# Four selective-scan layers on one core: x_dbl on both halves of the partitions, dt's projection of two blocks as one pair of matmuls, delta's second half by a transfer

## The chip, the cores and the metric

The kernel runs on one core of a Trainium2 chip. The metric is the device time of one launch in microseconds (us), which processes a batch of eight images. All data are float32.

## The reference

The reference takes x of shape 8 x 64 x 64 x 96 through four residual layers, `x = x + layer(groupnorm(x))`. Each layer is a Mamba block with 192 inner channels and 16 states: an input projection into xpart and z, a depthwise convolution (3x3 in layers 0 to 2, three causal taps in layer 3), SiLU, a selective scan over the 4096 pixels, a gate by silu(z) and an output projection. Layers 0 to 2 scan in four directions (rows and columns, each forwards and backwards; layer 1 in serpentine order) and have a layer norm ahead of the gate; layer 3 scans once. For one direction, cut to what matters:

```python
x_dbl = einsum('bdl,cd->bcl', xs, x_proj_w)          # rank + 16 + 16 rows
dts, B, C = split(x_dbl)
delta = softplus(einsum('brl,dr->bdl', dts, dt_proj_w) + dt_proj_b)
h = exp(delta_t * A) * h + (delta_t * u_t) * B_t     # per channel and state, step by step
y_t = sum over states of h * C_t;  y = y + D * u
```

The rank is 16 in layer 0 and 6 in the others.

## The kernel before, in words

A loop over the eight images holds the four layers, written out (`layer`, L165). A layer has a part ahead of the scans (normalisation, projection, convolution), the scans (`scans`, L600), and a part after them (norm, gate, output projection). The scans are most of the time.

**Chunks and steps.** A direction's 4096 positions are 8 chunks of 512 (CH). `walk` lists the pairs of direction and chunk in order: directions 0, 2, 1, 3 in layers 0 to 2 (32 chunks a layer), one direction in layer 3 (8 chunks). The 192 channels are three tiles t of 64. A tile of h has 64 channels times 2 states on its 128 partitions, so 16 states are 8 rows of scans, in two groups g of 4 (NH). One chunk is one step of 24 slots (SL), one scan each.

**One slot** (loop at L1019, m counts the slots): `scan` (L861) is DVE's recurrence over 512 positions, h = d_a * h + dbu. `decay` (L850), on ACT, computes d_a = exp(delta * A) four slots ahead. `enter` (L828), on PE, in every second slot, multiplies du by the diagonals of B, 16 matmuls on 64x64 tiles, for two scans. In every fourth slot `keep` (L881), on ACT, copies the last column of four scans as the next chunk's state, and `read_out` (L888), on POOL, then multiplies the four scans' h by C in place. `add_up` (L892), on PE, in the odd slots, sums h * C over the states. So six read-outs a step; the third belongs to g = 0, t = 2, the last to g = 1, t = 2.

**Preparation of the next chunk** is spread over the slots of a step by the dictionary `plan` (L935): slot -> functions, with how many chunks ahead they work. `project` (L659) makes x_dbl on PE (rows 0 to 15 C, 16 to 31 B, then a row for the bias and the rank's rows; in layers 0 to 2 the backward direction's rows too, on partitions from 64), for directions 0 and 1. `keep_x_dbl` (L670) copies it out of PSUM on ACT and issues transfers of it to memory: cm (C, which is read back with copies) and xm (all rows of the backward direction). For directions 2 and 3 `load_x_dbl` (L684) reads xm back. `turn_v` (L707) is dt's projection: for each of four blocks of 128 positions (every fourth one, `block`, L703) a matmul of x_dbl's block, as the stationary operand on 39 or 49 rows, with dt's weights gives v (positions on partitions, 192 + 16 columns); e counts pairs of blocks, each with a PSUM bank of its own, b the block in the pair. `turn_u` (L724) transposes u. `softplus` (L733), `keep_b` (L744) and `diagonals` (L780) are ACT's, `delta_of` (L750) and `du_of` (L761) DVE's, `diagonal` (L767) POOL's. `turn_back` (L805) turns delta_t back to channels on partitions, on PE: rows 0 to 127 (o = 0), and rows 128 to 191 (o = 1) twice, for both halves of the partitions. `keep_delta` (L817) copies the three tiles of delta out of PSUM on ACT: each of 64 rows, on both halves of the partitions. `spread_c` (L694) reads C of one group of states from memory with 64 copies of each row, two transfers of 512 KB. `load_u` (L649) reads u, 256 and 128 KB. `close_sums` (L913), on DVE, adds the chunk's sums to y.

**What sets the order.** The order of PE, DVE, ACT and POOL is the program's (`manual_schedule`, L218). SP issues all transfers, and its order is the tile framework's planner's, which goes by the time at which, by its reckoning, a transfer's inputs and buffer are ready, with the program's order as the priority. Buffers (L127 on): c 3, u 4, x_dbl 2, d_a 6, delta 6, and in PSUM 2 for dbu and 2 (`mm`) shared by x_dbl, v, u_t and delta_ps in turn. With three c buffers the second group's c of the next chunk takes the buffer that the third read-out of the present chunk has just read. The fourth u buffer comes free with close_sums of slot 14.

Of the kernel before, what the change touches and what calls it, by code (L numbers as in the profile page):

```python
# [22 lines left out]
F32 = mybir.dt.float32  # L23
# [7 lines left out]
DI = 192  # L31
NS = 16
# [3 lines left out]
CH = 512  # L36
# [128 lines left out]
def layer(tc, env, x, x_of, x_to, n, ly):  # L165
# [191 lines left out]
    def make_ys():  # L357
        return [big.tile([128, L], F32, tag=f"big{o}", name=f"y{o}") for o in range(2)]

    work = scans(  # L360
        tc, env, n, ly, w, u_mem, lambda half: u_chunk(half, 0), d, neg_a, make_ys, mm, wide
    )
# [237 lines left out]
def scans(tc, env, n, ly, w, u_mem, u_first, d, neg_a, make_ys, mm, wide):  # L600
# [7 lines left out]
    nc = tc.nc  # L608
    const, small = env.const, env.small
# [2 lines left out]
    R, K = ly.rank, ly.dirs  # L612
    XP = 33 + R
    RS, SL = 6, 24

    def mem(tag, k, rows):
        return env.dram.tile([rows, L], F32, tag=tag, name=f"{tag}{k}_{n}", bufs=2)
# [3 lines left out]
    x_mem = {k: mem("xm", k, XP) for k in range(2, K)}  # L621
# [5 lines left out]
    us, dbls, cs, diags, turned, rests, deltas = {}, {}, {}, {}, {}, {}, {}  # L627
# [10 lines left out]
    def bank(i, name, part=0):  # L638

        if i > 0:  # L640
            return mm(name)
        if part == 0:
            banks[name] = wide(name)
        return banks[name][:, part * CH : part * CH + CH]
# [25 lines left out]
    def keep_x_dbl(i):  # L670


        k, c = walk[i]
        if k >= 2:
            return
        s = slice(c * CH, (c + 1) * CH)
        x_dbl = small.tile([128, CH], F32, tag="x_dbl", name="x_dbl")[0 : ly.x_rows]
        nc.scalar.activation(x_dbl, dbls[i], AF.Identity, bias=const[0 : ly.x_rows, ONE : ONE + 1])
        nc.sync.dma_start(c_mem[k][:, s], x_dbl[0:NS])
        if K > 1:  # L680
            nc.sync.dma_start(x_mem[k + 2][:, s], x_dbl[64 : 64 + XP])
        dbls[i] = x_dbl[0:XP]

    def load_x_dbl(i):  # L684
        if i >= len(walk):
            return
        k, c = walk[i]
        if k < 2:
            return
        x_dbl = small.tile([128, CH], F32, tag="x_dbl", name="x_dbl")[0:XP]  # L690
        nc.sync.dma_start(x_dbl, x_mem[k][:, c * CH : (c + 1) * CH])
        dbls[i] = x_dbl

    def spread_c(i, g):  # L694
        k, c = walk[i]
# [7 lines left out]
    def block(b, ap):  # L703

        return ap[:, b::NB4]

    def turn_v(i, e, b):  # L707

        if e == 0 and b == 0:
            for name in ("delta_t", "du_t"):  # L710
                turned[i, name] = env.turned.tile([128, NB4, DI], F32, tag=name, name=name)
        if b == 0:
            v = bank(i, "v", e)[:, 0 : 2 * (DI + NS)]
            turned[i, e, "v"] = v.rearrange("p (b d) -> p b d", b=2)
        at = ly.dt_w + walk[i][0] * (DI + NS)
        nc.tensor.matmul(  # L716
            turned[i, e, "v"][:, b],
            block(2 * e + b, dbls[i]),
            w[0:XP, at : at + DI + NS],
            start=True,  # L720
            stop=True,
        )

    def turn_u(i, e, b):  # L724

# [78 lines left out]

    def turn_back(i, o, part):  # L805


        if part == 0:
            deltas[i, "ps", o] = bank(i, "delta_ps", o)
        for b in (2 * part, 2 * part + 1):  # L810
            of = turned[i, "delta_t"][:, b]
            for half in range(o + 1):
                to = deltas[i, "ps", o][64 * half : 64 * half + 128 // (o + 1)]
                of_ = of[:, 0:128] if o == 0 else of[:, 128:DI]
                nc.tensor.matmul(block(b, to), of_, ident, start=True, stop=True)  # L815

    def keep_delta(i, t):  # L817
        delta = env.deltas.tile([128, CH], F32, tag="delta", name="delta")
        if t == 2:
            nc.scalar.copy(delta, deltas[i, "ps", 1])  # L820
        else:
            for half in range(2):
                of = deltas[i, "ps", 0][64 * t : 64 * t + 64]
                nc.scalar.copy(delta[64 * half : 64 * half + 64], of)  # L824
        deltas[i, t] = delta
# [87 lines left out]
    def close_sums(i, o):  # L913
# [21 lines left out]
    plan = {  # L935
        0: [(load_u, 2)],
        1: [(keep_x_dbl, 1)],
        2: [(turn_v, 1, 0, 0)],
        3: [(turn_v, 1, 0, 1)],
        4: [(keep_b, 1, 0), (softplus, 1, 0, 0)],  # L940
        5: [(softplus, 1, 0, 1)],
        6: [(softplus, 1, 0, 2), (diagonal, 1, 0), (turn_u, 1, 0, 0), (spread_c, 1, 0)],
        7: [(turn_u, 1, 0, 1)],
        8: [(delta_of, 1, 0)],
        9: [(turn_v, 1, 1, 0)],
        10: [(diagonal, 1, 1), (turn_v, 1, 1, 1), (close_sums, -1, 0)],
        11: [(keep_b, 1, 1), (softplus, 1, 1, 0)],
        12: [(softplus, 1, 1, 1), (du_of, 1, 0)],
        13: [(softplus, 1, 1, 2), (turn_u, 1, 1, 0), (diagonal, 1, 2)],
        14: [(turn_u, 1, 1, 1), (close_sums, -1, 1)],  # L950
        16: [(delta_of, 1, 1), (spread_c, 1, 1)],
        17: [(turn_back, 1, 0, 0), (diagonal, 1, 3)],
        18: [(turn_back, 1, 0, 1), (du_of, 1, 1)],
        19: [(keep_delta, 1, 0), (load_x_dbl, 2)],
        20: [(turn_back, 1, 1, 0), (keep_delta, 1, 1)],
        21: [(turn_back, 1, 1, 1)],
        22: [(project, 2, 0)],
        23: [(project, 2, 1), (keep_delta, 1, 2)],
    }

    done = 0
    for slot, n_ in (
        *((10, 2), (14, 2), (15, 3), (16, 2), (17, 3), (18, 2), (21, 2), (22, 2)),
        *((24, 2), (25, 1), (26, 2), (27, 2), (28, 1), (29, 1), (30, 1), (31, 2), (32, 2)),
    ):
        plan.setdefault(slot % SL, []).append((diagonals, 1 - slot // SL, done, n_))
        done += n_


    def first_project():  # L970
        project(0, 0)
        project(0, 1)
        keep_x_dbl(0)
        for g in range(2):
            spread_c(0, g)

    def first_turn():
        for do in (turn_v, turn_u):
            for e in range(2):
                for b in range(2):  # L980
                    do(0, e, b)

    def first_softplus(between=lambda: None):
        for e in range(2):
# [21 lines left out]
    def first_load():  # L1006
# [3 lines left out]
    yield SimpleNamespace(  # L1010
        project=first_project,
        turn=first_turn,
        softplus=first_softplus,
        turn_back=first_back,
        keep_delta=first_delta,
# [3 lines left out]
    for m in range(-4, (len(walk) + 1) * SL):  # L1019
        i, slot = divmod(m, SL)  # L1020
# [9 lines left out]
        if slot % 2:  # L1030
            of, e = divmod(m - 13, SL)
# [26 lines left out]
def pack(ly, conv_w, win, conv_b, x_proj, dt_w, dt_b, a_log, d, w_out, gamma=None, beta=None):  # L1058
    K, R = ly.dirs, ly.rank
    XP = 33 + R  # L1060
    a = np.zeros((128, ly.width), np.float32)
    a[0:C, ly.win_x : ly.win_x + DI] = win[:DI].T
    a[0:C, ly.win_z : ly.win_z + DI] = win[DI:].T
    x_proj = x_proj.reshape(K, R + 2 * NS, DI)
    for k in range(K):

        w = x_proj[k].T
        at = ly.x_proj + k % 2 * 2 * ly.x_rows + k // 2 * 64
        for half, rows in enumerate((slice(0, 128), slice(128, DI))):
            to = a[0 : len(w[rows]), at + half * ly.x_rows : at + half * ly.x_rows + XP]  # L1070
            to[:, 0:NS] = w[rows, R + NS :]
            to[:, NS : 2 * NS] = w[rows, R : R + NS]
            to[:, 33:] = w[rows, :R]

        at = ly.dt_w + k * (DI + NS)
        a[32, at : at + DI] = dt_b.reshape(K, DI)[k]
        a[33:XP, at : at + DI] = dt_w.reshape(K, DI, R)[k].T
        for half in range(2):
            for j in range(NJ):
                a[NS + half * NJ + j, at + DI + j // NH * NJ + half * NH + j % NH] = 1  # L1080
    a_log = a_log.reshape(K * NT, 64, 2, NJ).transpose(2, 1, 0, 3).reshape(128, -1)
    a[:, ly.a_log : ly.a_log + K * NT * NJ] = a_log
    d = d.reshape(K, DI)
    a[:, ly.d : ly.d + K] = d[:, :128].T
    a[0:64, ly.d + K : ly.d + 2 * K] = d[:, 128:].T
    conv_w = conv_w.reshape(DI, ly.taps)
    a[:, ly.conv_w : ly.conv_w + ly.taps] = conv_w[:128]
    for p in (0, 64):
        a[p : p + 64, ly.conv_w + ly.taps : ly.conv_w + 2 * ly.taps] = conv_w[128:]
    for v, at in ((conv_b, ly.conv_b), (gamma, ly.gamma), (beta, ly.beta)):  # L1090
        if v is not None:
            a[:, at] = v[:128]
            a[0:64, at + 1] = a[64:128, at + 1] = v[128:]
    a[:, ly.w_out : ly.w_out + C] = w_out[:, :128].T
    for p in (0, 64):
        a[p : p + 64, ly.w_out + C : ly.w_out + 2 * C] = w_out[:, 128:].T
    return a
# [39 lines left out]
```

## Time and profile before

| what | value |
|---|---|
| median of 3 runs | 31,737.26 us (31,715.66 to 31,752.72) |
| the profiled execution's own time | 31,703.4 us |
| its span, first to last instruction | 31,698.6 us |
| PE busy | 30,814.0 us (97%) |
| DVE busy | 28,392.2 us (90%) |
| POOL busy | 27,178.5 us (86%) |
| ACT busy | 26,085.1 us (82%) |
| 16 DMA engines, share of their time | 33.3% in SP's queue |
| read_out, POOL, L890 | 4,992 x 4.557 us |
| scan, DVE, L872 | 19,968 x 1.20 to 1.26 us |
| decay, ACT, L858 | 19,968 x 0.716 us |
| turn_v, PE, L716 | 6,656 records, 8 a step |
| keep_delta, ACT, L824 and L820 | 3,328 x 0.580 us and 832 x 0.586 us |

A matmul of float32 leaves two records, each with a record of its weight load (PEld). Records of matmuls on different tiles of the array overlap, so what a matmul costs is read from start to next start. The clock granted to PE is 0.98 of full speed over the span. In a timeline, columns are start, duration, engine, line, operation, names, and in brackets the engine's idle time ahead of it and what ended it.

### The profile page before, as it was taken

What the parts mean: (1) busy time and instruction counts of PE and PEld (TensorE: products, weight loads), DVE (VectorE), ACT (ScalarE), POOL (GpSimd) and SP (SyncE); (2) the same over time, 40 slices, a digit from 0 to 9 for tenths busy, and PEclk for the clock granted to TensorE, in tenths of its full rate; (3) what the DMA queues carried; (4) which work ended last, traced back from release to release, by engine and by line L of the source; (5) the groups of instructions that cost most, each with busy time, mean ns of one, the idle gap of its engine ahead of it and who ended that gap; (6) DMA issues with size and microseconds to landing.
All of it is one profiled execution on the core that took longest, in us unless ns stands there. A gap on an engine that the chain in (4) does not pass through costs nothing. (4 is left out here: it accounts for less than half of the span.)

```text
span 31698.6 us, 951914 instructions
## 1 busy us (share of the span) xinstructions
PE 30814.0 (97%) x402320; PEld 16776.3 (53%) x402320; DVE 28392.2 (90%) x29432; ACT 26085.1 (82%) x65064; POOL 27178.5 (86%) x9436
## 2 busy tenths in 40 slices
PE   9999999999999999999999999999999999999999
PEld 5555555555555545555455554555555555555555
DVE  9899898998989989899898998989989899898998
ACT  8788788887888878888788887878878888788887
POOL 8898788987889879898798987989878898788987
PEclk9999999999999999999999999999999999999999
DMA  3333233333333333333333333333323333333332
GB/s 90 78 76 85 72 90 79 75 86 73 89 80 74 87 72 88 80 74 87 73 88 80 74 87 74 87 79 74 87 72 89 80 74 86 72 90 79 75 86 72
DMA packets 1262156, 2544.89 MB, mean 80 GB/s; under 512 B 108560, under 2 KB 129296, under 8 KB 1234832
## 3 DMA queue, kind: packets, MB, share of 16 engines
q1 hardware_dynamic: 1257872, 2483.64, 33.3%
q8 instruction: 3192, 52.30, 0.7%
q14 instruction: 1092, 8.95, 0.1%
HBM read 2208.74 MB, written 274.46 MB: 78 GB/s over the span
## 5 line engine op out<-in xcount | busy, mean ns | idle before, releaser
L890 POOL TENSOR_TENSOR h<-h,c 128x2048 f32<-128x2048 f32 x4992 | 22723.0, 4557 | 1867.5 <-ACT state L886 625.9
L872 DVE TENSOR_TENSOR_SCAN h<-d_a,state,dbu 128x512 f32<-128x512 f32 x17472 | 21076.5, 1261 | 1130.2 <-PE dbu L841 687.9
L858 ACT ACTIVATE d_a<-delta,neg_a 128x512 f32<-128x512 f32 x19968 | 14166.5, 716 | 122.1 <-DVE h L872 101.3
L841 PE MATMUL dbu<-diag,du_t 64*64 64x128 f32 x319488 | 11142.2, 277 | 296.4 <-DVE h L872 224.7
L841 PEld LDWEIGHTS dbu<-diag,du_t 64*64 64x64 f32 x319488 | 8712.0, 133 | 5111.5 <-issue 4681.5
L904 PE MATMUL y_ps<-h,const 128*64 128x512 f32 x39936 | 10827.0, 617 | 119.1 <-POOL h L890 110.5
L786 ACT ACTIVATE diag<-const,bt 128x64 f32<-128x64 f32 x25600 | 7550.4, 344 | 14.0 <-PE dbu L841 7.8
L773 POOL TENSOR_TENSOR diag<-const,bt 128x512 f32<-128x512 f32 x3328 | 3475.2, 1045 | 335.0 <-ACT bt L747 246.3
L872 DVE TENSOR_TENSOR_SCAN h<-d_a,dbu 128x512 f32<-128x512 f32 x2496 | 2881.8, 1203 | 498.6 <-ACT d_a L858 216.2
L904 PEld LDWEIGHTS y_ps<-h,const 128*64 128x64 f32 x39936 | 2065.6, 135 | 1899.4 <-issue 1498.5
L716 PE MATMUL v<-w,x_dbl 39*128 39x208 f32 (+1 forms) x6656 | 2618.4, 477 | 8.3 <-DVE delta_t L752 7.3
L716 PEld LDWEIGHTS v<-w,x_dbl 39*128 39x128 f32 (+1 forms) x6656 | 1787.2, 317 | 1568.3 <-issue 883.1
L824 ACT COPY delta<-delta_ps 64x512 f32<-64x512 f32 x3328 | 1930.9, 580 | 566.7 <-PE delta_ps L815 519.6
L815 PEld LDWEIGHTS delta_ps<-const,delta_t 128*64 128x64 f32 (+1 forms) x19968 | 1637.0, 154 | 1415.7 <-issue 949.7
L815 PE MATMUL delta_ps<-const,delta_t 128*64 128x128 f32 (+1 forms) x19968 | 2223.8, 286 | 11.6 <-issue 11.6
L747 ACT COPY bt<-v 128x32 f32<-128x32 f32 x1664 | 300.8, 183 | 1848.7 <-PE v L716 1846.5
L730 PEld LDWEIGHTS u_t<-const,u 128*128 128x128 f32 x3328 | 650.1, 195 | 1583.2 <-issue 887.2
L886 ACT COPY state<-h 128x4 f32<-128x4 f32 x4992 | 972.4, 195 | 568.0 <-DVE h L872 527.9
L454 POOL TENSOR_TENSOR acc<-acc,more 128x512 f32<-128x512 f32 x576 | 756.7, 1317 | 699.6 <-ACT more L453 356.1
L730 PE MATMUL u_t<-const,u 128*128 128x128 f32 x3328 | 1292.2, 388 | 0.0
L320 PE MATMUL conv<-xn,taps 96*128 96x512 f32 (+1 forms) x2496 | 1160.0, 658 | 22.1 <-DVE taps L203 22.1
L731 PE MATMUL u_t<-const,u 64*128 64x64 f32 x3328 | 1098.8, 330 | 0.0
(99 smaller groups left out, 16194.5 us busy)
## 6 DMA issues: line engine op xcount, KB each, us to landing
c<-cm SPq DMA_DIRECT2D x1792, 512.0 KB
c<-xm SPq DMA_DIRECT2D x1536, 512.0 KB
u<-u SPq DMA_DIRECT2D x1088, 256.0 KB
u<-u SPq DMA_DIRECT2D x1088, 128.0 KB
u<-u SPq DMA_DIRECT2D x48, 1024.0 KB
x_mem<-x SPq DMA_DIRECT2D x48, 768.0 KB
x<-x_mem SPq DMA_DIRECT2D x48, 768.0 KB
x<-in_x_dram SPq DMA_DIRECT2D x32, 768.0 KB
```

What stands on the lines that cost most here:

```text
L320: nc.tensor.matmul(part, taps[:, t, d0 : d0 + nd], rhs, start=t == 0, stop=t == ly.taps - 1)
L716: nc.tensor.matmul(turned[i, e, "v"][:, b], block(2 * e + b, dbls[i]), w[0:XP, at : at + DI + NS], start=True, stop=True,)
L730: nc.tensor.transpose(to[:, b, 0:128], block(b_, u_of(i, 0)), ident)
L773: nc.gpsimd.tensor_tensor(diags[i, 0][:, b], sel.unsqueeze(1).unsqueeze(3).to_broadcast([128, NH, 64, 2]), of.unsqueeze(2).to_broadcast([1 ...
L786: nc.scalar.activation(diags[i, 1][:, b, q // 2, :, q % 2], sel, AF.Copy, scale=turned[i, b // 2, "b"][:, b % 2, NJ + q : NJ + q + 1],)
L815: nc.tensor.matmul(block(b, to), of_, ident, start=True, stop=True)
L824: nc.scalar.copy(delta[64 * half : 64 * half + 64], of)
L841: nc.tensor.matmul(to[64 * half : 64 * half + 64, e, b], du[rows, b, 64 * t : 64 * t + 64], diag[rows, b, 2 * half + pair], start=True, st ...
L858: nc.scalar.activation(d_a, deltas[i, t], AF.Exp, scale=neg_a[:, at : at + 1])
L872: nc.vector.tensor_tensor_scan(hs[s][:, m4, flow], decays.pop(m)[:, flow], p[:, flow], 0.0 if first else states[i // NCH][:, j : j + 1], A ...
L890: nc.gpsimd.tensor_tensor(hs[s], hs[s], cs[i, g], ALU.mult)
L904: nc.tensor.matmul(sums[i][o][64 * half : 64 * half + 64], sel, hs[of][:, state, :], start=g == 0 and e in (0, 4), stop=g == 1 and e in (3 ...
```

## The change

x_dbl is kept on two places: on partitions 0 on, and on partitions 64 on. For directions 0 and 1 of a chunk after the first, a transfer makes the second place (x_hi, one buffer); for directions 2 and 3 a second load from xm does. `turn_v` then issues, for one b, the matmuls of both e, one on the rows from 0, one on those from 64, where dt's weights stand a second time. `turn_back` of rows 128 to 191 fills one half of the partitions. `keep_delta` copies each tile of 64 rows to one half only and issues a transfer of that half to the other. The plan deals the preparation anew. The first chunk of a layer has no second place and keeps the old way for delta.

```diff
@@ keep_x_dbl
         nc.scalar.activation(x_dbl, dbls[i], AF.Identity, bias=const[0 : ly.x_rows, ONE : ONE + 1])
+        dbls[i] = [x_dbl[0:XP], x_dbl[0:XP]]
+        if i > 0:
+            there = small.tile([128, CH], F32, tag="x_hi", name="x_hi", bufs=1)[64 : 64 + XP]
+            nc.sync.dma_start(there, x_dbl[0:XP])
+            dbls[i][1] = there
         nc.sync.dma_start(c_mem[k][:, s], x_dbl[0:NS])
         if K > 1:
             nc.sync.dma_start(x_mem[k + 2][:, s], x_dbl[64 : 64 + XP])
-        dbls[i] = x_dbl[0:XP]
@@ load_x_dbl
-        x_dbl = small.tile([128, CH], F32, tag="x_dbl", name="x_dbl")[0:XP]
-        nc.sync.dma_start(x_dbl, x_mem[k][:, c * CH : (c + 1) * CH])
-        dbls[i] = x_dbl
+        x_dbl = small.tile([128, CH], F32, tag="x_dbl", name="x_dbl")
+        dbls[i] = [x_dbl[o : o + XP] for o in (0, 64)]
+        for to in dbls[i]:
+            nc.sync.dma_start(to, x_mem[k][:, c * CH : (c + 1) * CH])
@@ turn_v, now turn_v(i, b)
-        nc.tensor.matmul(
-            turned[i, e, "v"][:, b],
-            block(2 * e + b, dbls[i]),
-            w[0:XP, at : at + DI + NS],
-            start=True,
-            stop=True,
-        )
+        for e, of in enumerate(dbls[i]):
+            o = 64 if i > 0 and e else 0
+            nc.tensor.matmul(
+                turned[i, e, "v"][:, b],
+                block(2 * e + b, of),
+                w[o : o + XP, at : at + DI + NS],
+                start=True,
+                stop=True,
+            )
@@ turn_back
-            for half in range(o + 1):
+            for half in range(o + 1 if i == 0 else 1):
@@ keep_delta
         delta = env.deltas.tile([128, CH], F32, tag="delta", name="delta")
-        if t == 2:
+        if i > 0:
+            here = halves[t % 2]
+            nc.scalar.copy(delta[here], deltas[i, "ps", t // 2][here])
+            nc.sync.dma_start(delta[halves[1 - t % 2]], delta[here])
+        elif t == 2:
             nc.scalar.copy(delta, deltas[i, "ps", 1])
@@ plan
         1: [(keep_x_dbl, 1)],
-        2: [(turn_v, 1, 0, 0)],
-        3: [(turn_v, 1, 0, 1)],
-        4: [(keep_b, 1, 0), (softplus, 1, 0, 0)],
-        5: [(softplus, 1, 0, 1)],
-        6: [(softplus, 1, 0, 2), (diagonal, 1, 0), (turn_u, 1, 0, 0), (spread_c, 1, 0)],
-        7: [(turn_u, 1, 0, 1)],
-        8: [(delta_of, 1, 0)],
-        9: [(turn_v, 1, 1, 0)],
-        10: [(diagonal, 1, 1), (turn_v, 1, 1, 1), (close_sums, -1, 0)],
-        11: [(keep_b, 1, 1), (softplus, 1, 1, 0)],
-        12: [(softplus, 1, 1, 1), (du_of, 1, 0)],
-        13: [(softplus, 1, 1, 2), (turn_u, 1, 1, 0), (diagonal, 1, 2)],
+        3: [(turn_v, 1, 0)],
+        4: [(turn_v, 1, 1)],
+        5: [(keep_b, 1, 0), (softplus, 1, 0, 0), (spread_c, 1, 0)],
+        6: [(softplus, 1, 0, 1), (softplus, 1, 0, 2), (diagonal, 1, 0)],
+        7: [(keep_b, 1, 1), (softplus, 1, 1, 0)],
+        8: [(delta_of, 1, 0), (softplus, 1, 1, 1)],
+        9: [(turn_u, 1, 0, 0), (softplus, 1, 1, 2)],
+        10: [(turn_u, 1, 0, 1), (diagonal, 1, 1), (close_sums, -1, 0)],
+        11: [(delta_of, 1, 1)],
+        12: [(du_of, 1, 0)],
+        13: [(turn_u, 1, 1, 0), (diagonal, 1, 2)],
         14: [(turn_u, 1, 1, 1), (close_sums, -1, 1)],
-        16: [(delta_of, 1, 1), (spread_c, 1, 1)],
-        17: [(turn_back, 1, 0, 0), (diagonal, 1, 3)],
-        18: [(turn_back, 1, 0, 1), (du_of, 1, 1)],
-        19: [(keep_delta, 1, 0), (load_x_dbl, 2)],
-        20: [(turn_back, 1, 1, 0), (keep_delta, 1, 1)],
-        21: [(turn_back, 1, 1, 1)],
+        15: [(turn_back, 1, 0, 0)],
+        16: [(turn_back, 1, 0, 1), (du_of, 1, 1), (spread_c, 1, 1)],
+        17: [(keep_delta, 1, 0), (diagonal, 1, 3)],
+        18: [(keep_delta, 1, 1)],
+        19: [(turn_back, 1, 1, 0), (load_x_dbl, 2)],
+        20: [(turn_back, 1, 1, 1)],
+        21: [(keep_delta, 1, 2)],
         22: [(project, 2, 0)],
-        23: [(project, 2, 1), (keep_delta, 1, 2)],
+        23: [(project, 2, 1)],
@@ slots and numbers of ACT's 32 diagonals (slots from 24 on are those of the chunk's own step)
-        *((10, 2), (14, 2), (15, 3), (16, 2), (17, 3), (18, 2), (21, 2), (22, 2)),
-        *((24, 2), (25, 1), (26, 2), (27, 2), (28, 1), (29, 1), (30, 1), (31, 2), (32, 2)),
+        *((10, 2), (11, 3), (12, 2), (13, 3), (14, 2), (15, 2), (16, 2), (19, 2), (20, 1), (22, 2)),
+        *((23, 2), (24, 1), (26, 2), (27, 2), (28, 2), (31, 1), (32, 1)),
@@ pack
+        a[64 : 64 + XP, at : at + DI + NS] = a[0:XP, at : at + DI + NS]
```

More of the change, by code (lines that the diff above doesn't have):

```diff
@@ L614, in scans @@
     RS, SL = 6, 24
+    halves = [slice(0, 64), slice(64, 128)]
     def mem(tag, k, rows):
@@ L705, in block, with turn_v @@
         return ap[:, b::NB4]
-    def turn_v(i, e, b):
-        if e == 0 and b == 0:
+    def turn_v(i, b):
+        if b == 0:
             for name in ("delta_t", "du_t"):
                 turned[i, name] = env.turned.tile([128, NB4, DI], F32, tag=name, name=name)
-        if b == 0:
-            v = bank(i, "v", e)[:, 0 : 2 * (DI + NS)]
-            turned[i, e, "v"] = v.rearrange("p (b d) -> p b d", b=2)
+            for e in range(2):
+                v = bank(i, "v", e)[:, 0 : 2 * (DI + NS)]
+                turned[i, e, "v"] = v.rearrange("p (b d) -> p b d", b=2)
         at = ly.dt_w + walk[i][0] * (DI + NS)
-        nc.tensor.matmul(
-            turned[i, e, "v"][:, b],
-            block(2 * e + b, dbls[i]),
-            w[0:XP, at : at + DI + NS],
-            start=True,
-            stop=True,
-        )
+        for e, of in enumerate(dbls[i]):
[7 more added lines that the diff above has]
+            )
     def turn_u(i, e, b):
@@ L977, in first_turn @@
     def first_turn():
[L978 to L981, printed above, removed]
+        for b in range(2):
+            turn_v(0, b)
+        for e in range(2):
+            for b in range(2):
+                turn_u(0, e, b)
     def first_softplus(between=lambda: None):
```

## The prediction

> **What bounds the kernel now.** First I read the busy shares of the page (PE 97%, DVE 90%, POOL 86%, ACT 82%): too close together to name one bound. So I timed the steps, by the start of every 24th scan on DVE. They are regular: 33.96 us where the chunk being prepared has x_dbl projected (directions 0 and 1), 33.53 in layer 3, 31.89 where x_dbl is loaded (directions 2 and 3). The 100 steps of an image that are followed by another (31 in each of three layers, 7 in the last) are 800 in the run and take 26,516.7 us, 33.15 on average, of 31,698.6. The change acts there. The engines' busy times over one step of each kind:
> ```profile
> 4670.64:4704.60 33.96, 33.96 (x477) 18.94 (x477) 31.51 (x30) 29.65 (x77) 31.28 (x11) 1.00 0.30 79
> 4934.92:4966.80 31.88, 31.88 (x474) 18.41 (x472) 31.40 (x31) 28.86 (x76) 31.15 (x11) 1.00 0.33 73
> ```
> Columns: stretch, its length, then PE, PEld, DVE, ACT, POOL, clock, DMA share, GB/s. PE is never idle and is the bound, but DVE and POOL stand within 0.5 to 0.8 us of it in the second kind. The timeline of PE around dt's projection:
> ```profile
> 4675.54 1.10 PE L841 MATMUL dbu<-diag,du_t 64*64 64x128 f32 x32
> 4676.57 0.79 PE L716 MATMUL v<-w,x_dbl 49*128 49x208 f32 x2
> 4677.30 1.08 PE L904 MATMUL y_ps<-h,const 128*64 128x512 f32 x4
> 4678.31 0.80 PE L716 MATMUL v<-w,x_dbl 49*128 49x208 f32 x2
> 4679.03 1.10 PE L841 MATMUL dbu<-diag,du_t 64*64 64x128 f32 x32
> ```
> From start to next start a v matmul costs 0.73 us, four a step. The second thing to see is the transfer queue. SP issues, in one step:
> ```profile
> 4694.30 1.23 SPq L700 DMA_DIRECT2D c<-cm  x2
> 4695.63 0.55 SPq L655 DMA_DIRECT2D u<-u  x1
> 4696.22 1.54 SPq L656 DMA_DIRECT2D u<-u  x1
> ```
> POOL tells why c goes out just then, and ACT what POOL waits for:
> ```profile
> 4689.70 4.57 POOL L890 TENSOR_TENSOR h<-h,c 128x2048 f32<-128x2048 f32 x1 [0.35 <-POOL diag L773]
> ...
> 4701.04 4.55 POOL L890 TENSOR_TENSOR h<-h,c 128x2048 f32<-128x2048 f32 x1 [0.26 <-ACT state L886]
> 4706.50 4.55 POOL L890 TENSOR_TENSOR h<-h,c 128x2048 f32<-128x2048 f32 x1 [0.92 <-PE y_ps L904]
> ```
> ```profile
> 4700.81 0.72 ACT L858 ACTIVATE d_a<-delta,neg_a 128x512 f32<-128x512 f32 x1
> 4701.55 1.18 ACT L824 COPY delta<-delta_ps 64x512 f32<-64x512 f32 x2
> ...
> 4706.17 0.20 ACT L886 COPY state<-h 128x4 f32<-128x4 f32 x1
> ```
> The third read-out of a step ends at 4694.27; call that moment t. It frees the c buffer, and c's second half for the next chunk is issued at t + 0.03. The first decay of the next chunk (4700.81) is six us later, and the state copy of 4706.17 must precede the last read-out (4706.50), which overwrites h. The table of waits has both dependencies in total:
> ```profile
> SPq L700 <- POOL h L890: 13914.7, 1475, 17.0
> POOL h L890 <- ACT state L886: 625.9, 1106, 5.2
> ```
> How long the queue is then full is in the DMA column:
> ```profile
> 4702.00:4704.00 2.00, 2.00 (x38) 1.26 (x38) 2.00 (x3) 1.96 (x6) 2.00 (x1) 1.00 0.72 221
> 4704.00:4706.00 2.00, 2.00 (x22) 0.66 (x14) 1.94 (x3) 1.98 (x5) 1.59 (x1) 1.00 0.00 0
> ```
> c and u are moved from 4696 to 4704. By the trace's completion records, over 656 steps: the second c transfer is complete 9.40 us after t, u's first 10.06, u's second (128 KB) 10.70 (9.74 to 11.93 in nine of ten).
>
> **What the Trainium skill says.** "DMA: Bandwidth & Descriptors", section "Queues, rings and completion order": SP owns one ring on each of the DMA engines, and an engine consumes its ring's descriptors in order. The trace agrees: u, issued 1.3 us after c, completes 0.66 us after it and not earlier. "TensorE: Matmul & The Clock Gate", Part 3 ("Packing small matmuls"): matmuls on different row groups run concurrently. Here the 32 records of a dbu group, 0.27 us each, fill 1.03 us on four 64x64 tiles. The same page, Part 1, "Architectural detail": ACT's queue is a strict FIFO; in the timelines here its instructions follow one another in the program's order.
>
> **The change, part by part.**
> - v for two blocks side by side: four matmuls of 0.73 become two pairs. If a pair takes as long as one, -1.45 us of PE a step; if it runs in sequence, 0. I take -1.45, on dbu's evidence.
> - turn_back of rows 128 to 191 to one half: 8 matmuls become 4. The 8 went as column pairs, so little is saved: 0.5 us a part now, 0.64 for the unpaired 128-row parts; between 0 and -0.5 a step, I take -0.05.
> - keep_delta: 4 copies of 580 ns and one of 586 become 3 of 580: -1.17 us of ACT a step. Added: three transfers of 128 KB on SP's queue (about 0.55 us of issue each, SP is free for most of a step) and, for every decay, a wait on their landing.
> - x_dbl's second copy, directions 0 and 1: one transfer ahead of cm and xm, which move back by one issue (0.3 us; c's first half, which needs cm, waits longer for POOL). A write of xm, the same rows, completes 1.93 us after issue (median; 3.13 at nine in ten). In the step shown SP issues cm at 4674.71, as soon as ACT ends x_dbl. Without a v in slot 2, slot 3's y_ps starts at 4676.57 and takes 1.01, so the pair is due at 4677.6. So 2.9 us stand against 1.9 to 3.2: cost 0, bounded by 0.3 us on such steps. What hides it is PE's work of slots 1 to 3; an ACT that comes late takes that away, and then dbu and y_ps queue behind the pair on PE, and DVE waits for dbu. x_hi has one buffer, free since the pairs of the step before have read it. Not less than 0: nothing waited for in slot 2 now goes away on the path. Directions 2 and 3: a second load next to the first, early in the step, 0.
> - The rest of the plan (u's transposes, softplus, diagonals: 32 on ACT as before, POOL's in the same slots): same work in other slots, 0 while PE, DVE and ACT have it in hand a slot before its reader. c's first half is asked for in slot 5 instead of 6, but waits for POOL's last read-out as before. The larger weights' rows: same transfer, 0.
> - **Delta by transfer, in the queue.** keep_delta(t=0) moves from slot 19 to 17, its reader, the first decay of the next chunk, stays in slot 20. SP's order is the planner's. It already puts the u load (slot 0 of the next step, buffer free at slot 14's close_sums) behind c (slot 16), so the planner holds c ready by slot 14; delta, ready at slot 17 at the earliest, then goes behind c, and likely behind u. It lands at t + 10.70 + 0.64 (another 128 KB, u1 to u2) = t + 11.34, with 0.1 for the signal D = t + 11.4. The other two transfers land behind, and are needed four and eight decays later: no wait. The first decay stands at t + 6.5 now. So ACT waits about 5 us, and behind it in ACT's order are, up to the state copy: four decays at 0.62 from start to start, five diagonals at 0.235, one delta copy at 0.55 = 4.2 us. State copy to read-out start is 0.33. So the last read-out starts at t + 15.95, and POOL, which is free at t + 11, idles. From there POOL's own chain runs to the next t: four read-outs at 4.51 and two diagonals at 1.0 = 20.1. **The loop closes at 36.05 us**, for both kinds of step, whatever PE saves: PE (32.5 or 30.4), DVE (31.4) and POOL (31.2) all fit within.
>
> Sum: 800 x 36.05 = 28,840 against 26,516.7: +2,323 us. On the profiled execution's 31,703.4 us that is 34,027; the median of the runs lies 34 us above that execution, so **34,060 us**. Last steps of a layer and all before the scans stay as they are.
>
> **The rivals.**
> 1. The loop, but delta ahead of u in SP's order: D = t + 9.40 + 0.64 + 0.1 = t + 10.15, period 34.8, 800 x 34.8 = 27,840, time 33,060. For it: program order. Against: the planner's readiness (it already lets the x_dbl load of slot 19 go ahead of c of slot 16).
> 2. **Faster:** delta gets ahead of c in SP's queue, or lands early for another reason, and the loop stays open. Then PE's saving counts: steps with projection 33.96 - 1.5 = 32.5, the others fall to DVE's 31.4 with some 0.2 for friction, 31.6. 52 of the former at -1.4 and 48 of the latter at -0.3 (now 31.89) make -88 us an image, -704 in all: 31,030. It decides at D: the period is D - t + 24.65, equal to the present mean of 33.15 at D = t + 8.5. Against it: c alone takes 9.40.
> 3. The pairs do not run side by side: alone, no gain and no loss (31,700); with the loop nothing is changed, since PE has 2 us to spare.
> 4. ACT's lateness reaches x_dbl, and PE waits for its second copy in slot 3: in the loop, keep_x_dbl ends 2.2 us after the state copy's start (a state copy, two decays, a diagonal and itself), at D + 6.4, and the copy lands at D + 8.4; scans then end about 1.7 us ahead of POOL's need. It adds up to 0.3 us to some steps, within the range.
>
> **How the numbers follow.** Loop with u ahead of delta (34,060): 0.60. Loop without (33,060): 0.15. A shorter loop, slower yet than now (31,800 to 32,700): 0.05. Open loop, faster: 0.18. Within 0.2%, about what a measurement of this kernel can tell from no change, and rival 3 with an open loop: 0.02; rival 4 lies within the loop's cases. The first case's own spread is the landing's, -0.4 to +0.7 us a step, 33,750 to 34,600. A range of 32,500 to 34,700 holds the first two and most of the third, 0.79.
>
> **What would show it.** Right: steps of one length, near 36, in both kinds; ACT's decay waiting for the delta transfer some 5 us a step; POOL's last read-out waiting for ACT's state copy; PE with 3 to 5 us idle in a step; v pairs at about 0.75 us. Wrong: SP's order with delta ahead of c; steps of 32.5 and 31.6; no ACT wait on the transfer.

## The result, and the profile after

The changed kernel takes 35,533.39 us (median of 4 runs, 35,515.51 to 35,554.03) against 31,740.61 us of the kernel before in the same session (4 runs): ratio 1.1196, 95% interval 1.1179 to 1.1212. It is slower, as forecast, but by 3,793 us and not by 2,323: the time lies 833 us above the top of the range.

| us | before | after |
| --- | --- | --- |
| span of the profiled execution | 31,698.6 | 35,535.1 |
| the 800 steps of the prediction | 26,516.7 (33.15 each) | 30,293.7 (37.87 each) |
| all the rest | 5,181.9 | 5,241.4 |
| clock granted to TensorE, of full speed | 0.980 | 0.932 |

So 3,777 of the 3,837 us more are in the steps. On the page of the changed kernel, the busy times of the engines are close to what they were, but their shares are not, and two groups have long waits ahead of them (after the bar: busy time, mean, then the idle time and what ended it):
```profile
PE 31916.4 (90%) x395920; PEld 16858.1 (47%) x395920; DVE 28475.2 (80%) x29432; ACT 25186.5 (71%) x63464; POOL 27089.7 (76%) x9436
...
L871 ACT ACTIVATE d_a<-delta,neg_a 128x512 f32<-128x512 f32 x19968 | 14186.6, 715 | 4909.5 <-DMA delta<-delta 4859.3
...
L725 PE MATMUL v<-w,x_hi 39*128 39x208 f32 (+1 forms) x1664 | 803.1, 575 | 776.1 <-DMA x_hi<-x_dbl 773.3
```
The decays wait for the delta transfer 4,859.3 us, 6.1 us a step. Before, they hardly waited at all:
```profile
L858 ACT ACTIVATE d_a<-delta,neg_a 128x512 f32<-128x512 f32 x19968 | 14166.5, 716 | 122.1 <-DVE h L872 101.3
```
The second wait, of PE for x_hi, is the one that the prediction priced at almost nothing.

One step with projection, in the order of the loop. SP's issues in the changed kernel; the third read-out ended at 5236.07, this is t:
```profile
5236.10 1.24 SPq L706 DMA_DIRECT2D c<-cm  x2
5237.43 0.55 SPq L656 DMA_DIRECT2D u<-u  x1
5238.03 1.45 SPq L657 DMA_DIRECT2D u<-u  x1
5240.22 11.36 SPq L831 DMA_DIRECT2D delta<-delta  x3
```
The order is c, u, delta, as forecast. ACT, same stretch:
```profile
5242.56 0.19 ACT L899 COPY state<-h 128x4 f32<-128x4 f32 x1
5248.91 0.72 ACT L871 ACTIVATE d_a<-delta,neg_a 128x512 f32<-128x512 f32 x1 [6.16 <-DMA delta<-delta]
...
5253.19 0.18 ACT L899 COPY state<-h 128x4 f32<-128x4 f32 x1
```
and POOL:
```profile
5243.24 4.51 POOL L903 TENSOR_TENSOR h<-h,c 128x2048 f32<-128x2048 f32 x1
5253.50 9.01 POOL L903 TENSOR_TENSOR h<-h,c 128x2048 f32<-128x2048 f32 x2 [5.74 <-PE dbu L854]
```
The first decay starts at t + 12.84; four decays, five diagonals and a delta copy later comes the state copy, and 0.31 us after its start POOL's last read-out, which had been due at 5247.75. (POOL's wait is put down to PE; the state copy is what ends last before it.) Before, the same read-out followed its predecessor with 0.92 us between.

PE, in the step ahead of it:
```profile
5216.44 0.80 PE L725 MATMUL v<-w,x_dbl 49*128 49x208 f32 x2
5218.94 0.80 PE L725 MATMUL v<-w,x_hi 49*128 49x208 f32 x2 [1.70 <-DMA x_hi<-x_dbl]
...
5220.70 0.56 PE L725 MATMUL v<-w,x_dbl 49*128 49x208 f32 x1
5220.70 0.56 PE L725 MATMUL v<-w,x_hi 49*128 49x208 f32 x1
...
5221.53 1.98 PE L917 MATMUL y_ps<-h,const 128*64 128x512 f32 x4
```
The second pair does run side by side: both its matmuls start at 5220.70, and the next group follows 0.83 us later. In the first pair the x_hi half starts 2.50 us behind the x_dbl half, and PE idles for 1.70 us of that, because ACT was late with x_dbl and the copy takes its 2.6 us after that.

The lengths of the steps, from t to the next t, and where delta's first transfer lands and the first decay stands in them (means; first steps of a layer and layer 3 are left out):

| preparation in the step | steps | before | after | delta lands, after t | first decay, after t |
| --- | --- | --- | --- | --- | --- |
| with projection, u in the queue | 336 | 34.01 | 38.86 | 12.28 | 12.37 |
| loaded x_dbl, u in the queue | 288 | 32.28 | 37.36 | 12.39 | 12.47 |
| loaded x_dbl, no u (end of a layer) | 96 | 31.43 | 34.42 | 10.12 | 10.21 |

### The profile page after: what moved, and what is told of

The parts are those of the page before. It is cut to its first block, busy times and chain, and to the rows that moved or that the text cites. A ratio compares the mean times of both kernels' runs of the same rounds, so it can differ in the third digit from the quotient of the medians.

```text
span 35535.1 us, 946898 instructions
## 1 busy us (share of the span) xinstructions
PE 31916.4 (90%) x395920; PEld 16858.1 (47%) x395920; DVE 28475.2 (80%) x29432; ACT 25186.5 (71%) x63464; POOL 27089.7 (76%) x9436
## 3 DMA queue, kind: packets, MB, share of 16 engines
q1 hardware_dynamic: 1492464, 2867.38, 35.9%
## 5 line engine op out<-in xcount | busy, mean ns | idle before, releaser
L871 ACT ACTIVATE d_a<-delta,neg_a 128x512 f32<-128x512 f32 x19968 | 14186.6, 715 | 4909.5 <-DMA delta<-delta 4859.3
L854 PE MATMUL dbu<-diag,du_t 64*64 64x128 f32 x319488 | 11762.6, 286 | 1971.9 <-DVE h L885 1701.8
L854 PEld LDWEIGHTS dbu<-diag,du_t 64*64 64x64 f32 x319488 | 9261.2, 139 | 7730.6 <-issue 6499.1
L917 PE MATMUL y_ps<-h,const 128*64 128x512 f32 x39936 | 11975.4, 648 | 158.6 <-POOL h L903 118.9
L917 PEld LDWEIGHTS y_ps<-h,const 128*64 128x64 f32 x39936 | 2323.3, 140 | 2401.4 <-issue 1669.2
L823 PEld LDWEIGHTS delta_ps<-const,delta_t 128*128 128x128 f32 (+1 forms) x13568 | 1619.5, 163 | 1437.2 <-issue 1432.7
L823 PE MATMUL delta_ps<-const,delta_t 128*128 128x128 f32 (+1 forms) x13568 | 2211.6, 290 | 26.0 <-issue 26.0
L725 PE MATMUL v<-w,x_dbl 39*128 39x208 f32 (+1 forms) x4992 | 1501.1, 520 | 209.7 <-ACT x_dbl L679 207.5
L830 ACT COPY delta<-delta_ps 64x512 f32<-64x512 f32 x2400 | 1389.9, 579 | 312.1 <-PE delta_ps L823 258.8
L725 PEld LDWEIGHTS v<-w,x_dbl 39*128 39x128 f32 (+1 forms) x4992 | 933.2, 316 | 1261.7 <-ACT x_dbl L679 511.2
L725 PE MATMUL v<-w,x_hi 39*128 39x208 f32 (+1 forms) x1664 | 803.1, 575 | 776.1 <-DMA x_hi<-x_dbl 773.3
```

The lines of the kernel that those rows point to most:

```text
L725: nc.tensor.matmul(turned[i, e, "v"][:, b], block(2 * e + b, of), w[o : o + XP, at : at + DI + NS], start=True, stop=True,)
L830: nc.scalar.copy(delta[here], deltas[i, "ps", t // 2][here])
L854: nc.tensor.matmul(to[64 * half : 64 * half + 64, e, b], du[rows, b, 64 * t : 64 * t + 64], diag[rows, b, 2 * half + pair], start=True, st ...
L871: nc.scalar.activation(d_a, deltas[i, t], AF.Exp, scale=neg_a[:, at : at + 1])
L917: nc.tensor.matmul(sums[i][o][64 * half : 64 * half + 64], sel, hs[of][:, state, :], start=g == 0 and e in (0, 4), stop=g == 1 and e in (3 ...
```

## The experiments

All were timed against the kernel before on the same chip; e1 to e4 and e5 to e8 each ran together. Theory A is the loop of the prediction. Every edit is to the changed kernel, except e3's.

**e1: delta's second half by ACT, as before; everything else changed.**
```diff
@@ turn_back
-            for half in range(o + 1 if i == 0 else 1):
+            for half in range(o + 1):
@@ keep_delta
-        if i > 0:
-            here = halves[t % 2]
-            nc.scalar.copy(delta[here], deltas[i, "ps", t // 2][here])
-            nc.sync.dma_start(delta[halves[1 - t % 2]], delta[here])
-        elif t == 2:
+        if t == 2:
```


> The changed kernel with delta's second half copied by ACT again, as before the change (and turn_back's rows 128 to 191 twice); x_dbl on both halves, the pairs and the new plan stay. Theory A (the loop through c, delta's landing, ACT's order and POOL): the loop is gone, steps with projection fall to about 32.7 us and the others to 31.6, total 31,000 to 31,300 us. Rival B (the new plan, x_hi's landing and PE's idle spells cost the time by themselves): still above 34,000.

Measured: 31,599.94 us, ratio 0.9964 (0.995 to 0.9978). The whole loss goes with the transfer, but the time lies 300 us above Theory A's range, and the gain on the kernel before is far smaller than rival 2's 704 us. Steps with projection take 33.57 us, the others 32.02 (31.18 without u). The first steps of the four layers take 41.6, 35.6, 41.0 and 33.2 us against 37.3, 31.2, 35.3 and 31.0 before, some 130 us in all; PE waits 218.5 us for x_hi in this run, in 40 places. In the other steps with projection PE idles for 0.88 us, against 0.14 before.

**e2: the transfer stays, but c's second half is issued behind delta's second transfer.**
```diff
@@ keep_delta
-            nc.sync.dma_start(delta[halves[1 - t % 2]], delta[here])
+            sent[0] = nc.sync.dma_start(delta[halves[1 - t % 2]], delta[here])
@@ spread_c(i, 1) for i > 0
+            with tc.issue_after(sent[0].ins):
@@ plan
-        16: [(turn_back, 1, 0, 1), (du_of, 1, 1), (spread_c, 1, 1)],
+        16: [(turn_back, 1, 0, 1), (du_of, 1, 1)],
-        18: [(keep_delta, 1, 1)],
+        18: [(keep_delta, 1, 1), (spread_c, 1, 1)],
```


> The changed kernel with only SP's order changed: c's second half is issued behind delta's first two transfers (slot 18 instead of 16), delta still goes by transfer. Theory A: delta t=0 lands some 2 to 3 us after its copy, before the first decay reads it, the loop is open, total 31,000 to 31,500 us. Rival C (a transfer from half to half is too slow for three slots wherever it stands in the queue): ACT still waits 2 us and more a step, total above 33,500.

Measured: 31,350.03 us, ratio 0.9883 (0.9866 to 0.9899). The same transfers with the same bytes, only in another order, and the loss is a gain. SP in a step of this kernel, in which t is 4645.50:
```profile
4648.99 1.71 SPq L838 DMA_DIRECT2D delta<-delta  x2
4650.74 1.29 SPq L713 DMA_DIRECT2D c<-cm  x2
```
In steps with projection delta lands on average 6.2 us after t, 2.4 us after its issue, and the first decay stands at t + 6.4 (6.9 before the change); with loaded x_dbl it stands at t + 6.0 (6.2). The edit moves u as well: SP no longer stands at c's wait, issues u at about t in steps with projection, and u is complete at about the time at which delta is issued. So neither long transfer is ahead of delta. It is the place in the queue that costs, not the transfer: 4,180 us between these two orders.

**e3: the kernel before, with only delta's second half by transfer.** No second place of x_dbl, no pairs, the old plan.
```diff
@@ turn_back
-            for half in range(o + 1):
+            for half in range(o + 1 if i == 0 else 1):
@@ keep_delta
-        if t == 2:
+        if i > 0:
+            here = halves[t % 2]
+            nc.scalar.copy(delta[here], deltas[i, "ps", t // 2][here])
+            nc.sync.dma_start(delta[halves[1 - t % 2]], delta[here])
+        elif t == 2:
```


> The kernel before with delta's second half by transfer (and turn_back once) and nothing else: old plan, v one by one, no x_hi. Theory A: the same loop, D at t + 12.3, then four decays, two copies and four diagonals, 4.5 us, and 20.4 to the next t: about 37.3 us in every step, total some 35,000 us. Rival B: the transfer alone costs little, under 32,500.

Measured: 35,602.1 us (one run). The transfer alone is enough for a loss of this size, somewhat more than I expected. It is not made up of the same parts: in the old plan the second delta copy is placed behind the first decay, so that its transfer is issued only after the wait and lands at t + 15.7; a second wait follows the first (steps 38.08 us with u, 34.84 without, 39.07 with projection).

**e4: the delta transfers issued from ACT.** In the trace their packets are in a queue of their own (q10), c's and u's in q1.
```diff
-            nc.sync.dma_start(delta[halves[1 - t % 2]], delta[here])
+            nc.scalar.dma_start(delta[halves[1 - t % 2]], delta[here])
```


> The changed kernel with delta's transfers issued from ACT instead of SP, so that they stand in a ring of their own, while c and u are in flight on SP's. Theory A with rings that share each DMA engine in turns: delta lands 2.5 to 4 us after its copy, the loop opens almost or quite, total 31,000 to 32,300 us. If all rings of an engine drain in order of issue (rival D): as the changed kernel, about 35,500.

Measured: 35,686.02 us, ratio 1.1252 (1.1233 to 1.127). The own queue gains nothing: delta is issued 2.0 to 4.5 us after t and lands at 11.4 to 12.1 with u about, at 9.9 without. The little that it lands earlier is lost again, since ACT now issues a transfer between the first decay and the state copy: from first decay to last read-out it takes 5.23 us instead of 4.58. Two timelines of this kernel, SP's and then ACT's; here t is 5024.08:
```profile
5024.11 1.24 SPq L706 DMA_DIRECT2D c<-xm  x2
5025.45 0.55 SPq L656 DMA_DIRECT2D u<-u  x1
```
```profile
5025.87 0.47 ACTq L831 DMA_DIRECT2D delta<-delta  x1
...
5037.35 0.72 ACT L871 ACTIVATE d_a<-delta,neg_a 128x512 f32<-128x512 f32 x1 [7.80 <-DMA delta<-delta]
```
In the packet records of that stretch the first packet of ACT's queue starts at 5032.22, over six us after its issue, when some 490 of c's 512 packets of 2 KB have started; from then on its packets run mixed with u's. The queue is not slow by itself: its third transfer of a step, issued when c and u have landed, lands 2.19 us after issue. So the wait is for c, as on SP's queue. The landings go by the order of issue across both queues, as rival D has it: in 335 of the 336 steps with projection of the table c, u's two parts and delta land in the order in which SP and ACT issued them (in 170 of 240 with loaded x_dbl, where the issues lie close together), and in 34 steps with loaded x_dbl in which ACT issues delta ahead of both parts of u it lands at t + 10.0, ahead of u's first part at t + 11.1.

**e5: u behind delta's three transfers.** Delta then has only c ahead of it.
```diff
@@ keep_delta
-            nc.sync.dma_start(delta[halves[1 - t % 2]], delta[here])
+            sent[0] = nc.sync.dma_start(delta[halves[1 - t % 2]], delta[here])
@@ load_u, both transfers
+        with tc.issue_after(sent[0].ins) if sent else ExitStack():
```


> Theory A (closed loop, its period set by what stands between the third read-out and delta's landing): with u behind delta's three transfers, delta has only c ahead of it. In the last steps of a layer of the changed kernel, which have no u ahead, delta lands 10.1 us after the read-out and the step is 34.4 us; so the steps with loaded x_dbl go from 37.4 to about 34.4, those with projection from 38.9 to about 36 (they keep what they lose to x_hi), 700 steps at -2.8: 33,570 us, between 33,400 and 33,900. Theory B (the length of the whole queue counts, in whatever order): the same bytes in flight, delta lands at 12.3 as before, about 35,500 us.

Measured: 33,668.46 us, ratio 1.0608 (1.0592 to 1.0625), within A's range. Delta lands at t + 9.84 with loaded x_dbl and 10.02 with projection, 2.55 and 2.26 us earlier than in the changed kernel, and the steps are 2.72 and 2.97 us shorter (34.64 and 35.89). The period follows the landing nearly one for one, while a step moves the same bytes. With it rival 1 has been run in effect: it forecast a landing of 10.15 and steps of 34.8.

**e6: x_hi by a second ACT activation from PSUM, not by a transfer;** delta's transfers stay.
```diff
@@ keep_x_dbl
-        dbls[i] = [x_dbl[0:XP], x_dbl[0:XP]]
+        ps, dbls[i] = dbls[i], [x_dbl[0:XP], x_dbl[0:XP]]
@@ the same, x_hi
-            nc.sync.dma_start(there, x_dbl[0:XP])
+            nc.scalar.activation(
+                there, ps[0:XP], AF.Identity, bias=const[0:XP, ONE : ONE + 1]
+            )
```


> x_hi is written by a second ACT activation from PSUM and not by a transfer; the delta transfers stay. Theory A (rival 4 of the prediction, too small there: in the loop PE waits for x_hi's landing, then runs at a lower clock): the wait of PE on x_hi goes, the steps with projection fall from 38.9 to the 37.4 of the others, 390 steps at -1.5, and the first steps of a layer lose some 3 us each: about 34,900 us, between 34,750 and 35,050. Theory B (these steps are longer for PE's projection itself): the wait goes elsewhere, 35,500 us, or 35,700 with 0.6 us more on ACT inside the loop.

Measured: 34,815.21 us, ratio 1.0967 (1.095 to 1.0984): 718 us less than the changed kernel, and steps with projection of 37.63 us against 38.86. PE in such a step:
```profile
5157.17 0.80 PE L727 MATMUL v<-w,x_dbl 49*128 49x208 f32 x2 [1.03 <-ACT x_dbl L679]
5157.88 0.80 PE L727 MATMUL v<-w,x_hi 49*128 49x208 f32 x2
...
5160.58 1.98 PE L919 MATMUL y_ps<-h,const 128*64 128x512 f32 x4
```
PE still waits for x_dbl itself, 1.03 us, but no more for its copy. Its clock still drops after that (the y_ps group takes 1.98 us; the granted clock is 0.95 of full speed over the step, 0.96 in the changed kernel's), and yet POOL's second read-out follows the first by 5.5 us and not by 6.9. So x_hi's wait was the cost, and the lower clock, which I had suspected, was not. ACT's extra activation (0.68 us) lies inside the loop and shows: from first decay to the next step's first read-out it takes 9.67 us instead of 9.17.

**e7: e2 and e6 together**, the loop open and x_hi by ACT.

> Delta ahead of c as in the best kernel so far (31,350 us, loop open), and x_hi by ACT. In that kernel's steps PE never waits for x_hi within a layer, but the first steps of a layer are 42.9, 35.9, 41.0 and 33.1 us against 37.3, 31.2, 35.3 and 31.0 in the kernel before. Theory A (x_hi's transfer costs only in these first steps): 32 steps at -4, some -140 us: 31,210 us, between 31,150 and 31,280. Theory B (the first steps wait for delta or c, not for x_hi): 31,350. Theory C (ACT's extra 0.6 us in steps with projection counts): 31,450 to 31,600.

Measured: 31,194.06 us, ratio 0.983 (0.9817 to 0.9844), the fastest kernel here, 1.7% under the kernel before. The first steps of the layers fall from 42.9, 35.9, 41.0 and 33.1 us in e2 to 37.3, 31.2, 36.4 and 30.0; over 8 images that makes -144 us, of -156 measured against e2. One step with projection and one without:
```profile
4596.79:4629.96 33.17, 32.59 (x470) 17.90 (x468) 31.50 (x32) 29.22 (x76) 31.12 (x11) 1.00 0.41 99
4885.24:4916.45 31.21, 30.88 (x468) 17.46 (x464) 31.21 (x31) 27.83 (x74) 31.21 (x11) 1.00 0.38 86
```
With projection PE works 32.59 of 33.17 us; without, POOL and DVE are busy throughout. This is rival 2's picture (32.5 for PE, 31.4 for DVE). It forecast 31,030, 164 us too little: the steps with projection take 33.34 us on average, from scan to scan, and PE idles for 0.64 of them, against 0.14 before. Its waits for DVE's scans, which free dbu's PSUM buffers, have grown in the new plan; the kernel before and e2:
```profile
PE dbu L841 <- DVE h L872: 224.7, 423, 4.8
PE dbu L861 <- DVE h L892: 631.9, 1204, 4.8
```
Which part of the new plan makes it wait no run here separates.

**e8: e2 with v one matmul after the other**, both from the first place of x_dbl; no second place, no x_hi.
```diff
@@ keep_x_dbl
-        if i > 0:
-            there = small.tile([128, CH], F32, tag="x_hi", name="x_hi", bufs=1)[64 : 64 + XP]
-            nc.sync.dma_start(there, x_dbl[0:XP])
-            dbls[i][1] = there
@@ load_x_dbl
-        dbls[i] = [x_dbl[o : o + XP] for o in (0, 64)]
-        for to in dbls[i]:
-            nc.sync.dma_start(to, x_mem[k][:, c * CH : (c + 1) * CH])
+        dbls[i] = [x_dbl[0:XP], x_dbl[0:XP]]
+        nc.sync.dma_start(x_dbl[0:XP], x_mem[k][:, c * CH : (c + 1) * CH])
@@ turn_v
-            o = 64 if i > 0 and e else 0
+            o = 0
```


> Delta ahead of c (loop open), but v one matmul after the other, both from the first place of x_dbl; no second place, no x_hi. It prices the pairs where PE counts. Theory A (a pair takes what one takes, 0.73 us, so PE has 1.46 us more a step): steps with projection, which PE bounds, go from 33.2 to 34.6; the others, which POOL and DVE bound at 31.2 while PE works 30.7, to 32.2; 400 x 1.4 and 400 x 0.9 make +920, less some 140 in the layers' first steps, which need not wait for x_hi: 32,130 us, ratio 1.013. Theory B (the pairs save little and the gain of the best kernel comes from the new deal of the preparation): 31,200 to 31,350, ratio 0.986.

Measured: 31,823.56 us, ratio 1.0029 (1.0019 to 1.004), between the two theories. Without the pairs nothing of the gain is left, so A's cause holds, but its size was too large. PE's timelines say why, here e8's and then a pair of e7's:
```profile
4698.42 1.26 PE L727 MATMUL v<-w,x_dbl 49*128 49x208 f32 x4
4699.61 1.10 PE L856 MATMUL dbu<-diag,du_t 64*64 64x128 f32 x32
```
```profile
4603.35 0.56 PE L734 MATMUL v<-w,x_dbl 49*128 49x208 f32 x1
4603.35 0.56 PE L734 MATMUL v<-w,x_hi 49*128 49x208 f32 x1
...
4604.08 1.10 PE L863 MATMUL dbu<-diag,du_t 64*64 64x128 f32 x32
```
Two matmuls one after the other in one slot take 1.19 us, not twice 0.73; in e7 a pair side by side takes 0.73. A pair saves 0.46 us, two of them 0.92 a step. Measured against e7, which is the fairer neighbour since it too has no transfer of x_hi, the steps with projection are 0.94 us longer (34.28 against 33.34 on average), the others 0.75. Against the kernel before, PE spends 0.52 us less on v in a step with projection, and yet the step is not shorter (34.28 against 34.21): here too PE idles for 0.67 us of it. The new plan takes back what it saves there.

## Why the prediction was right in kind and too small in size

What held: c, u, delta is SP's order; the first decay waits for delta's landing; behind it in ACT's order is the state copy that POOL's last read-out needs; from there to the next t it is POOL's chain; PE's saving counts for nothing in the loop. First decay to last read-out was put at 4.53 us and is 4.58. From last read-out to the next t, put at 20.1, it is 20.31 in steps with loaded x_dbl. (The terms written out in the prediction add up to 35.97 us, not 36.05, 60 us over all steps; and its range, from 32,500 on, holds the smaller part of the third case, 31,800 to 32,700, and not most of it.) Rival 3 is refuted by the pair records and by e8. Rival 2's open loop is what happens when delta is ahead of c (e2, e7) or not in the queue at all (e1), with less gain than it forecast. One sign did not come: the steps are not of one length, those with projection are 1.5 us longer (38.86 against 37.36).

Two terms of the sum were too small.

1. **D, the landing and its signal: t + 11.4 forecast, t + 12.4 to 12.5 measured (first decay).** The step that failed was taking the completion times of before, with delta's 0.64 us added on top. The 0.64 is right (0.61 to 0.65). But c and u themselves complete later, once delta stands behind them. The completion of c's second half after t, by what is issued behind it, from the traces of before, e1, e3, e5 and after (means over steps; e5 against after differs in the order alone):

| behind c while it is moved | c complete, us after t |
| --- | --- |
| nothing | 8.99 (before), 9.14 (e1) |
| two delta transfers, 256 KB | 9.29 (e5), 9.52 (after, no u) |
| u, 384 KB | 9.39 (before), 9.49 (e1) |
| u and one delta, 512 KB | 9.73 (e3) |
| u and two deltas, 640 KB | 10.11 (after) |

 c's issue is the same in all rows (t + 0.03 and t + 0.65). So c gives 0.7 of the missing 1.0 us and u the rest. Over the 624 steps with u outside layer 3 this is some 640 us, and the chain behind, 0.25 us longer than in the sum, another 150. The 112 steps without u, at 34.4 to 34.8 and not 36.05, give back some 180.

2. **Rival 4, "up to 0.3 us to some steps": some 1.5 us in steps with projection, and more in a layer's first.** The chain up to PE was the right one, state copy, x_dbl, copy, PE. ACT ends x_dbl 6.55 us after the first decay (6.4 forecast); the copy lands 2.5 us later and not 2.0. What failed is the path from there to POOL: rival 4 follows the delay through dbu and DVE's scans alone and lets their lead over POOL absorb it. ACT waits for v too, to copy B's rows out of it (`keep_b`), and behind that in ACT's order stands the state copy that the second read-out needs. In the step shown, ACT and then POOL:
```profile
5221.63 0.18 ACT L756 COPY bt<-v 128x32 f32<-128x32 f32 x1 [1.37 <-PE v L725]
...
5224.98 0.19 ACT L899 COPY state<-h 128x4 f32<-128x4 f32 x1
```
```profile
5225.32 4.55 POOL L903 TENSOR_TENSOR h<-h,c 128x2048 f32<-128x2048 f32 x1 [0.93 <-ACT state L899]
```
In all 336 steps with projection of the table this read-out starts 0.33 us after the state copy does, and POOL idles for 1.63 us before it. The scans do come late, but on average still end 0.48 us before POOL is free (3.2 us before in e6, more than the 1.7 assumed); ACT's wait for v is 2.04 us. So the two read-outs start 6.90 us apart instead of 5.5. In e6, without the wait for x_hi, ACT waits 0.04 us for v and POOL not at all, and 718 us are gained. Half of the miss of 1,473 us is this wait; the landing, the chain and what the steps without u give back make 610 us, everything outside the 800 steps 60. Some 85 us are not assigned.

The prediction said that x_hi's transfer is hidden by PE's work of slots 1 to 3 and that a late ACT takes that away. In the main case it then made ACT late by five us a step and still priced the cover as if it were there. A cover that the likeliest case itself removes belongs into that case's sum.

That c's completion grows with what stands behind it is shown. Why is left open: a DMA engine that ends its part of c early may begin on the next transfer and slow the others, but no run here separates that from other causes.

## What to carry to other kernels

A transfer that replaces a copy has the price of its place in the queue, so look for what was issued just ahead of it, and put the short one that an in-order engine waits for ahead of the long one that nobody needs soon: the order alone was worth 4,180 us here. When a landing sets the period, do not simply add a transfer's duration to the completion times of a trace without it: here the transfers ahead were delayed too. When the likeliest case makes an engine late, go through the steps that counted on that engine as cover and price them again. And follow a late result to every engine that reads it, not only along the path with the most work: here ACT's short copy of v held up the state copy behind it.

## What the runs showed of the hardware that was not expected

- **Another queue did not let a transfer past.** The Trainium skill, "DMA: Bandwidth & Descriptors", section "Queues, rings and completion order", says that each engine goes round between the queue rows that have work, packet by packet. In e4 no such sharing is seen while c is moved: delta on ACT's queue starts over six us after its issue, when some 490 of c's 512 packets have started, and c, u and delta land in the order of issue across both queues (335 of 336 steps with projection). The measurement decides for this case. The section gives a packet as typically 9 to 17 descriptors and at most 64; how many c's packets hold no run here shows, and why the order of issue counts isn't settled.
- **Completion gets later with what is queued behind**: 8.99 us with nothing behind c, 10.11 with 640 KB, as in the table above.
- **Two matmuls next to one another cost less than two apart**: 1.19 us for two v matmuls in one slot (e8), 0.73 for each one that stands alone between other groups (before), 0.73 for a pair on two row groups (e7). Of the 1.45 us a step that the pairs were forecast to save, which is what e7 shows, 0.53 come from putting two in one slot and 0.92 from running them side by side. This is PE's time; of the 0.53 nothing was left in the length of e8's steps.
- **PE's clock fell for a short while, and that did not cost**: in the steps shown of the changed kernel and of e6 the granted clock is half of full speed for 3.4 us after PE's waits (1.70 and 1.03 us, and others before them), and the y_ps group takes 1.98 us instead of 1.08. Only where x_hi is waited for do the read-outs come later. How much waiting makes the clock fall was not tested.
